# Expert tiles behind the second recurrence: the down weights of a tile copied by ScalarE instead of GpSimd

## The chip, the cores and the metric

One core of a Trainium2 chip runs the whole program. The metric is device time in microseconds (us) of one execution. The kernel before took 3821.63 us, the median of 13 runs that lay between 3815.52 and 3829.98.

## The reference, cut to what matters

Two layers work on x of shape (8, 512, 256). The change touches the last sub-block alone: a simple recurrence over 512 steps, and behind it a mixture of experts in which each of the 4096 rows goes to the best 2 of 16 experts. All is float32.

```python
h_next = jnp.tanh(xw_t + h_prev @ Wh)                     # 512 steps in a row
...
router_logits = jax.nn.sigmoid(x @ gate_w + gate_b)
expert_values, expert_indices = jax.lax.top_k(router_logits, k=2)
expert_values = expert_values / jnp.sum(expert_values, axis=-1, keepdims=True)
...                                                       # for each expert e:
all_outputs[e] = (silu(x @ experts_wg[e]) * (x @ experts_wu[e])) @ experts_wd[e]
return x + shared_mlp(x) + sum_of_the_two(expert_values * selected_outputs)
```

An expert's weights are gate and up (256 by 128 each) and down (128 by 256).

## The kernel before, in words

The last sub-block is `rnn_moe`. Its main loop issues the 512 recurrence steps; each step also advances by one piece whatever else is at hand, taken from generators: the ranking of routed rows (`ranks`), the collection of finished experts' rows (`gathers`), the chunks of 16 steps that compute router and shared expert (`chunks`), and long work (`big`), to which the expert tiles belong. When the recurrence is over, a second loop goes on with the same generators, a slot at a time, until all are empty. That second loop is what this document calls the tail.

The rows are treated in four blocks of 9, 9, 9 and 5 chunks of 128 rows. For each block `rank` gives every row a place in its expert's group, padded to tiles of 128 rows, and scatters the rows to DRAM (`xs`, line L1720, one indirect DMA of GpSimd for each of the two experts of a chunk). `tiles` then works through 33 tiles (25 in the last block). `collect` gathers the results back (L1830, two indirect DMAs of GpSimd for each chunk), adds them on VectorE (L1838) and stores the output.

In `tiles`, each tile m belongs to one expert, and its number is known only on the chip. `whose` (L1740) loads the numbers of four tiles into registers of GpSimd with one instruction. `fetch(m)` allocates a tile `w` of 768 columns from a pool of **4 buffers** and copies the expert's weights into it from the SBUF tensors that hold all 16 experts: gate and up, 512 columns (L1751), then down, 256 columns (L1752), both on GpSimd. TensorE reads `w` at fixed places.

One tile takes three slots. `later(f)` puts work aside until the next slot begins; then `consume` issues it in the order in which it was put aside. With tile m in its three slots, this is issued:

| slot | TensorE | at the start of the next slot |
|---|---|---|
| 1 | gate(m) (L1771), transpose of half of x(m+2) (L1761) | ScalarE sigmoid(m) (L1780), VectorE multiply (L1781) |
| 2 | up(m) (L1771), transpose of the other half | VectorE multiply (L1781), ScalarE copy xT(m+2) (L1765) |
| 3 | down(m-1) (L1787); then `fetch(m+4)` and the load of x(m+5) are issued | ScalarE copy y(m-1) (L1791) and its store to `ys` |

So the numbers m+4 of `fetch` and m-1 of `down` stand in the same slot: w(m+4) is issued while down(m), the last reader of the buffer that w(m+4) takes over, is issued one tile later.

All this lies within `manual_schedule` for TensorE, ScalarE and VectorE: these three run their instructions in the order in which they are issued above. The order on GpSimd and SyncE (loads and stores) is set by the framework's scheduler. The framework places all waits: the first writers of a tile wait until the last reader of the buffer's former tile is done. The PSUM results of gate and up (`pg`) have 2 buffers, those of down (`py`) 2, the transposed x (`pt`) one.

Of the kernel before, what the change touches and what calls it, by code (L numbers as in the profile page):

```python
# [22 lines left out]
D = 256  # L23
# [1489 lines left out]
def rnn_seed(K, M, t, j):  # L1513

    pick = M.pick[:, t % XB : t % XB + 4].rearrange("p t b -> p (t b)")
    xw = M.xw[:, t // XB - 1] if t >= XB else M.xw0
    K.nc.tensor.matmul(M.pg[t // 4 % 2][32 * j : 32 * j + 32], pick, xw[:, 64 * j : 64 * j + 64], start=True, stop=True)


def rnn_step(K, M, t):  # L1520


    nc, mm = K.nc, K.nc.tensor.matmul
    at, now = t % XB, t % 4
    if at == 0:
        M.last, M.ring = M.ring, M.rings[t // XB % 3]
    pg = M.pg[t // 4 % 2]
    for k in range(2):
        if t == 0:
            hp = K.h0T[:, k, :]  # L1530
        elif now == 0:
            first = B + (at or XB) * 64 - 64 + 32 * k + 24
            hp = (M.ring if at else M.last)[:, first : first + B]
        else:
            first = at * 64 - 64 + 32 * k
            hp = M.ring[:, first : first + B * (now + 1)]
        for j in range(4):
            mm(pg[32 * j : 32 * j + B * (now + 1)], hp, M.wh[:, k, 64 * j : 64 * j + 64], start=False, stop=(k == 1), skip_group_check=True)  # L1538
    h = M.hp.tile([P, 64], F32, name="h", tag="h")
    nc.scalar.activation(h, pg, AF.Tanh)  # L1540
    M.pace = nc.vector.transpose(M.ring[:, B + 64 * at : B + 64 * at + 64], h)  # L1541


class Experts:
# [187 lines left out]
    def tiles(self):  # L1732

        K, M, NT = self.K, self.M, self.NT
        nc, mm, later = K.nc, K.nc.tensor.matmul, M.later
        W, X, A, T = {}, {}, {}, {}

        def whose(m):
            n = min(4, NT - m)
            _, v = nc.values_load_multi_w_load_instructions(  # L1740
                self.wrow[0:1, m : m + n], engines=[mybir.EngineType.Pool], min_val=0, max_val=self.NE - 1,
                skip_runtime_bounds_check_because="the expert is a count, limited to NE - 1 by a minimum", bass_reorder=False,
            )
            for i in range(n):
                W[m + i] = v[i]

        def fetch(m):
            if m % 4 == 0:
                whose(m)
            e, W[m] = bass.ds(W[m], 1), M.wp.tile([P, 768], F32, name="w", tag="w")  # L1750
            nc.gpsimd.tensor_copy(W[m][:, 0 : 2 * D], M.wgu[:, e, :].rearrange("p o n -> p (o n)"))  # L1751
            nc.gpsimd.tensor_copy(W[m][:, 2 * D : 3 * D], M.wdn[:, e, :].rearrange("p o n -> p (o n)"))  # L1752

        def rows(m):
            X[m] = M.sp.tile([P, D], F32, name="x", tag="x", bufs=5)
            nc.sync.dma_start(out=X[m], in_=self.xs[m * P : (m + 1) * P, :])

        def turn(m, k):
            if k == 0:
                T[m] = M.pxt.tile([P, 2, P], F32, name="pt", tag="xt")  # L1760
            nc.tensor.transpose(T[m][:, k, :], X[m][:, k * P : (k + 1) * P], K.ident)  # L1761
            if k == 1:
                pt, xT = T.pop(m), M.sp.tile([P, 2, P], F32, name="xT", tag="xT")
                X[m] = xT
                later(lambda: nc.scalar.copy(xT, pt))  # L1765

        def gate(m, g):

            pg = M.pgu.tile([P, P], F32, name="pg", tag="gu")
            for k in range(2):  # L1770
                mm(pg, W[m][:, k * D + g * P : k * D + (g + 1) * P], X[m][:, k, :], start=(k == 0), stop=(k == 1))  # L1771
            if g == 0:
                A[m] = M.sp.tile([P, P], F32, name="ea", tag="ea")
            else:
                X.pop(m)
            a = A[m]

            def part():
                if g == 0:
                    nc.scalar.activation(a, pg, AF.Sigmoid)  # L1780
                nc.vector.tensor_tensor(a, pg, a, ALU.mult)  # L1781

            later(part)

        def down(m):
            py = M.pd.tile([P, D], F32, name="py", tag="pd")
            M.last = mm(py, A.pop(m), W.pop(m)[:, 2 * D : 3 * D], start=True, stop=True)  # L1787

            def keep():
                y = M.sp.tile([P, D], F32, name="y", tag="y")  # L1790
                nc.scalar.copy(y, py)  # L1791
                nc.sync.dma_start(out=self.ys[m * P : (m + 1) * P, :], in_=y)

            later(keep)

        for m in range(4):
            fetch(m)
            rows(m)
        rows(4)
        for _ in range(5):  # L1800
            yield 0
        for m in range(2):
            for k in range(2):
                turn(m, k)
            yield 1
        for m in range(NT + 1):
            if m < NT:
                for n in range(2):
                    gate(m, n)
                    if m + 2 < NT:  # L1810
                        turn(m + 2, n)
                    yield 1
            if m:
                down(m - 1)
            if m + 4 < NT:
                fetch(m + 4)
            if m + 5 < NT:
                rows(m + 5)
            yield 1
# [26 lines left out]
def rnn_moe(K, out, start):  # L1846


    nc, inp, mm = K.nc, K.inp, K.nc.tensor.matmul
    with ExitStack() as es:  # L1850
        wp = K.pool(es, "m_w")
        M = Scope()
# [59 lines left out]
        def consume():  # L1912
            now = due[:]
            due.clear()
            for f in now:
                f()

        def advance(queue):

            while queue:  # L1920
                used = next(queue[0], None)
                if used is not None:
                    return used
                queue.pop(0)
            return 0
# [13 lines left out]
        def chunk(x, c, ring):  # L1939
            yield from x.chunk(c, ring)  # L1940
            if c == x.C - 1:
                ranks.append(ranked(x))

        M.left = True
        nb, at = -1, 0
        with K.tc.manual_schedule(engines={E.PE, E.Activation, E.DVE}):
            for t in range(S):
                if t % XB == 0:
                    if t == XB * sum(BLOCKS[: nb + 1]):
                        nb += 1  # L1950
                        block, at = Experts(K, M, nb), 0
                rnn_step(K, M, t)
                consume()
                advance(ranks)
                advance(gathers)
                idle = not (advance(chunks) or advance(big))
                if idle:
                    mm(M.pgu.tile([P, P], F32, name="fill", tag="gu"), K.ident, M.wx[:, 0, 0:P], start=True, stop=True)
                for j in ((0, 1), (2,), (3,), ())[t % 4]:
                    if t // 4 * 4 + 4 < S:  # L1960
                        rnn_seed(K, M, t // 4 * 4 + 4, j)
                if t % XB == XB - 1:
                    chunks.append(chunk(block, at, M.ring))
                    at += 1
            while chunks or ranks or big or gathers:
                consume()
                M.left = bool(chunks or ranks or big)
                advance(ranks)
                advance(gathers)
                if advance(chunks) or advance(big):  # L1970
                    M.pace = M.last
            consume()
# [179 lines left out]
```

## Time and profile before

The profiled execution took 3815.2 us; its span (first to last instruction) is 3813.4 us.

| what | where read | value |
|---|---|---|
| busy share of the span | first part of the page | TensorE 90%, VectorE 62%, ScalarE 42%, GpSimd 17% |
| last step of the recurrence (L1540) begins | timeline of ScalarE | 3662.91 us |
| tail | the rest | some 150 us, to 3813.4 |
| GpSimd weight copies (L1751, L1752) | groups of the tail alone | 54 of each; 643 and 446 ns on average |
| GpSimd indirect DMAs in the tail | the same | 46 gathers of 971 ns, 10 scatters of 1042 ns |
| ScalarE busy in the tail | groups of the tail | copies xT and y 58 times 372 ns each, sigmoid 58 times 277 ns |

In a timeline line the first two numbers are start and duration in us; brackets hold the idle time of the engine before it and what ended it. A group line ends with busy time, mean ns of one, and idle time before. "f32 x4" of a matmul means four passes that the profile counts as instructions; a float32 matmul of the program takes two.

### The profile page before, as it was taken

How to read it: one execution, taken by the hardware profiler on the slowest of the kernel's cores; microseconds unless marked ns; L12 is line 12 of the kernel's file. 1: busy time of each engine (PE TensorE's matmuls, PEld its weight loads, DVE VectorE, ACT ScalarE, POOL GpSimd, SP SyncE). 2: the span in 40 equal slices, each digit the busy share in tenths (PEclk: the TensorE clock that was granted, in tenths of full speed). 3: DMA queues.
4: the chain of work that ended last, by engine and by line, in shares of the span. 5: the costliest groups of instructions: out<-in, count | busy, mean ns of one | idle time of the engine just before them, and what ended most of it. 6: DMA issues, size and time to landing. Idle time of an engine off the chain costs nothing.

```text
span 3813.4 us, 146239 instructions
## 1 busy us (share of the span) xinstructions
PE 3413.8 (90%) x62442; PEld 2298.6 (60%) x62442; DVE 2372.4 (62%) x8871; ACT 1617.0 (42%) x5695; POOL 661.5 (17%) x1479
## 2 busy tenths in 40 slices
PE   8999888888888888789999999999999999999986
PEld 5533455555565555556656666666666666676765
DVE  4488667767777777656767666666667633344444
ACT  3111255555555555445544444444444412233334
POOL 1000000000000000000013223222222210225466
PEclk9899999999999999999999999999999999999999
DMA  3022100000000000120000000000000033123345
GB/s 113 24 83 72 35 19 20 22 17 22 5 5 5 5 5 5 31 70 26 10 3 1 2 1 1 1 2 1 1 7 1 1 129 96 50 64 98 98 131 166
DMA packets 102924, 137.91 MB, mean 36 GB/s; under 512 B 12336, under 2 KB 84048, under 8 KB 102144
## 3 DMA queue, kind: packets, MB, share of 16 engines
q1 hardware_dynamic: 88416, 89.03, 7.5%
q0 software_dynamic: 11040, 34.29, 2.8%
q8 instruction: 490, 8.03, 0.9%
q10 hardware_dynamic: 2816, 5.24, 0.4%
q14 instruction: 162, 1.33, 0.1%
HBM read 86.44 MB, written 43.25 MB: 34 GB/s over the span
## 4 chain that ended last, share of the span: by engine, by line
PE 66%; ACT 14%; DVE 12%; issue 5%; POOL 2%; DMA 1%; ACTq 0%; SPq 0%; POOLq 0%; DVEq 0%
PE pgf L678 5%; PE pe L1245 4%; PE pg L1538 4%; PE pt L1288 3%; DVE G L684 3%; PE po L1303 3%; PE pg L1771 3%; PE U L489 3%; PE pp L1205 3%; PE px L1324 3%; PE pk L468 3%; ACT th L694 3%; ACT so L685 2%; ACT left L685 2%; ACT right L685 2%
## 5 line engine op out<-in xcount | busy, mean ns | idle before, releaser
L678 PE MATMUL pgf<-wh,ring 128*16 128x64 f32 x8176 | 215.2, 223 | 201.7 <-DVE ring L695 199.0
L678 PEld LDWEIGHTS pgf<-wh,ring 128*16 128x16 f32 x8176 | 127.4, 99 | 393.8 <-DVE ring L695 393.8
L1265 ACT ACTIVATE sm<-sm,nm 128x388 f32<-128x388 f32 (+3 forms) x512 | 283.5, 555 | 180.1 <-DVE nm L1261 179.9
L1541 DVE STREAM_TRANSPOSE ring<-h 128x64 f32<-128x64 f32 x512 | 125.5, 245 | 345.0 <-ACT h L1540 338.4
L685 ACT ACTIVATE sf<-G 128x16 f32<-128x16 f32 x512 | 110.5, 216 | 462.5 <-DVE G L684 462.5
L1540 ACT ACTIVATE h<-pg 128x64 f32<-128x64 f32 x512 | 114.3, 223 | 400.8 <-PE pg L1538 396.9
L1290 ACT COPY eT<-pt 128x512 f32<-128x512 f32 (+1 forms) x192 | 105.5, 549 | 354.4 <-PE pt L1288 354.1
L1288 PE MATMUL pt<-ident,sm 128*128 128x128 f32 x1280 | 191.8, 281 | 56.2 <-DVE sm L1271 42.2
L1205 PE MATMUL pp<-hn,wqkv 128*128 128x512 f32 x512 | 238.5, 609 | 0.8 <-DVE xT L932 0.8
L1538 PE MATMUL pg<-down,ring 128*16 128x64 f32 x8176 | 230.6, 223 | 6.6 <-DVE ring L1541 4.6
L1288 PEld LDWEIGHTS pt<-ident,sm 128*128 128x128 f32 x1280 | 147.0, 142 | 138.8 <-issue 83.2
L1272 POOL COPY pme<-sm 128x4 f32<-128x4 f32 x512 | 119.1, 234 | 640.2 <-DVE sm L1271 635.9
L678 PE MATMUL pgo<-wh,ring 128*16 128x64 f32 x8176 | 216.5, 220 | 15.3 <-issue 14.8
L678 PE MATMUL pgg<-wh,ring 128*16 128x64 f32 x8176 | 211.5, 220 | 4.7 <-issue 4.5
L637 POOL COPY xc<-xT 128x128 f32<-128x128 f32 x64 | 16.9, 293 | 1135.2 <-DVE xT L552 1061.8
L684 DVE STREAM_TRANSPOSE G<-pgf 128x64 f32<-128x64 f32 x512 | 127.5, 249 | 137.2 <-PE pgf L678 131.2
L678 PE MATMUL pgi<-wh,ring 128*16 128x64 f32 x8176 | 209.5, 219 | 0.9 <-issue 0.8
L1261 DVE CUSTOM_DVE_ANT_0 sm<-pe,mask 128x260 f32<-128x260 f32 (+2 forms) x384 | 141.8, 425 | 85.5 <-PE pe L1245 81.8
L1771 PE MATMUL pg<-xT,w 128*128 128x128 f32 x992 | 167.4, 295 | 18.8 <-POOL w L1751 17.2
L1271 DVE TENSOR_SCALAR sm<-sm,rc 128x388 f32<-128x388 f32 (+3 forms) x512 | 176.0, 387 | 9.0
L695 DVE TENSOR_TENSOR ring<-so,th 128x16 f32<-128x16 f32 x512 | 90.0, 176 | 147.1 <-ACT th L694 147.1
L643 PE MATMUL px<-wx,xc 128*128 128x256 f32 x512 | 173.2, 422 | 5.1 <-POOL xc L637 5.0
(534 smaller groups left out, 8178.5 us busy)
## 6 DMA issues: line engine op xcount, KB each, us to landing
cb<-order POOLq DMA_DIRECT2D x32, 512.0 KB
x<-xs SPq DMA_DIRECT2D x124, 128.0 KB
ys<-y SPq DMA_DIRECT2D x124, 128.0 KB
xs<-zero SPq DMA_DIRECT2D x66, 128.0 KB
w<-in_ada_w_dram SPq DMA_DIRECT2D x16, 512.0 KB
w<-in_moh_w_dram SPq DMA_DIRECT2D x32, 195.0 KB
xres<-xp SPq DMA_DIRECT2D x32, 128.0 KB
xc<-xres SPq DMA_DIRECT2D x32, 128.0 KB
```

Of the source, the lines that this page charges most:

```text
L643: mm(px, xc[:, k], wx[:, k, c], start=(k == 0), stop=(k == 1))
L678: mm(dst[32 * j : 32 * j + B * (now + 1)], hp, w, start=False, stop=(k == 1), skip_group_check=True)
L684: nc.vector.transpose(G.rearrange("p k b -> p (k b)"), banks[n][0])
L685: nc.scalar.activation(to, G[:, :, B * now : B * now + B], f)
L1205: mm(pp, T.wqkv[:, k, 0 : 2048].rearrange("p (i g h n) -> p i g h n", i=2, g=4, h=2)[:, i, g, h], self.hn[b][:, k, :], start=(k == 0), sto ...
L1245: mm(pe[a][:, 0 : w - lo], q[r, h, at], k[r, h, lo:w], start=(h == 0), stop=(h == 1))
L1261: nc.vector.tensor_tensor_reduce(out=sm[a][:, lo:w], in0=pe[a][:, 0 : w - lo], in1=T.mask[:, S - n + lo : 4 + S], scale=-1.0 / 8.0, scalar ...
L1265: nc.scalar.activation(sm[a][:, 0:w], sm[a][:, 0:w], AF.Exp, bias=nm[:, a : a + 1], scale=-1.0, accum_out=su[:, a : a + 1])
L1271: nc.vector.tensor_scalar(sm[a][:, 0:w], sm[a][:, 0:w], rc[:, a : a + 1], None, ALU.mult)
L1288: nc.tensor.transpose(pt[:, at, :], sm[i * m + a][:, 4 + j * P : 4 + (j + 1) * P], K.ident)
L1538: mm(pg[32 * j : 32 * j + B * (now + 1)], hp, M.wh[:, k, 64 * j : 64 * j + 64], start=False, stop=(k == 1), skip_group_check=True)
L1771: mm(pg, W[m][:, k * D + g * P : k * D + (g + 1) * P], X[m][:, k, :], start=(k == 0), stop=(k == 1))
```

## The change

In the tail, `fetch` leaves the copy of the down weights to ScalarE. A flag `M.tail` is set between the two loops. `whose`, when called in the tail, loads the four expert numbers into a register of ScalarE as well as of GpSimd, and notes for these tiles that both have it. For a noted tile `fetch` copies gate and up on GpSimd as before, and puts the copy of the down weights aside with `later`, so that ScalarE issues it at the start of the next slot, behind the copy y(m-1) that was put aside just ahead of it. Tiles whose numbers were loaded before the tail are fetched as before.

```diff
-                self.wrow[0:1, m : m + n], engines=[mybir.EngineType.Pool], min_val=0, max_val=self.NE - 1,
+                self.wrow[0:1, m : m + n], engines=[mybir.EngineType.Pool] + [mybir.EngineType.Activation] * M.tail, min_val=0, max_val=self.NE - 1,
...
                 W[m + i] = v[i]
+                both[m + i] = M.tail
...
             nc.gpsimd.tensor_copy(W[m][:, 0 : 2 * D], M.wgu[:, e, :].rearrange("p o n -> p (o n)"))
-            nc.gpsimd.tensor_copy(W[m][:, 2 * D : 3 * D], M.wdn[:, e, :].rearrange("p o n -> p (o n)"))
+            last, kept = W[m][:, 2 * D : 3 * D], M.wdn[:, e, :].rearrange("p o n -> p (o n)")
+            if both[m]:
+                later(lambda: nc.scalar.copy(last, kept))
+            else:
+                nc.gpsimd.tensor_copy(last, kept)
...
-        M.left = True
+        M.left, M.tail = True, False
...
+            M.tail = True
             while chunks or ranks or big or gathers:
```

More of the change, by code (lines that the diff above doesn't have):

```diff
@@ L1735, in tiles @@
         nc, mm, later = K.nc, K.nc.tensor.matmul, M.later
-        W, X, A, T = {}, {}, {}, {}
+        W, X, A, T, both = {}, {}, {}, {}, {}
         def whose(m):
```

## The prediction

> **What bounds the kernel now.** I read the waits of the weight copy first, then the windows and timelines of the tail. The tail runs from 3663 us to the end; the third and the fourth block of tiles (33 and 25) lie in it, and only there does the change act. In its window GpSimd is the busiest engine, 111.11 of 150 us, and TensorE has 106.85:
>
> ```profile
> 3663.00:3813.00 150.00, 106.85 (x722) 91.00 (x721) 64.91 (x200) 59.99 (x178) 111.11 (x166) 0.91 0.57 168
> ```
>
> The copies y, one for each tile on ScalarE, are the clock of the tiles. These four lines are y(0) and y(29) of the third block and y(0) and y(21) of the last (counted from each block's end):
>
> ```profile
> 3672.47 0.37 ACT L1791 COPY y<-py 128x256 f32<-128x256 f32 x1
> ...
> 3737.09 0.37 ACT L1791 COPY y<-py 128x256 f32<-128x256 f32 x1
> ...
> 3745.16 0.37 ACT L1791 COPY y<-py 128x256 f32<-128x256 f32 x1
> ...
> 3787.65 0.37 ACT L1791 COPY y<-py 128x256 f32<-128x256 f32 x1
> ```
>
> So 29 tiles took 64.62 us and 21 took 42.49. From 3722 to 3738 a tile takes 1.54 us and TensorE never pauses; elsewhere GpSimd's indirect DMAs stand between the weight copies, TensorE waits for w (43.4 us in 42 waits in the whole run), and a tile takes 2.0 to 2.7 us. GpSimd is thus the bound of about two thirds of the tail's tiles, and the change takes work off it. What matters is where ScalarE must do it. The waits ahead of the gate and up copy show what a weight copy itself waits for:
>
> ```profile
> L1751 POOL COPY w<-xT x124: 603/614/872, 3274.2 to 3786.2; 128x512 f32 x124
> ...
> its engine sat idle before it (us, times) until:
>   PE py L1787: 163.5, 61
> ```
>
> It waits for a down matmul, the last reader of its buffer. The timeline of the last tiles shows which one, and what ScalarE does meanwhile:
>
> ```profile
> 3784.57 0.37 ACT L1791 COPY y<-py 128x256 f32<-128x256 f32 x1
> ...
> 3784.97 0.28 ACT L1780 ACTIVATE ea<-pg 128x128 f32<-128x128 f32 x1
> ...
> 3785.43 0.60 PE L1787 MATMUL py<-w,ea 128*128 128x256 f32 x2
> ...
> 3786.11 0.37 ACT L1791 COPY y<-py 128x256 f32<-128x256 f32 x1
> 3786.16 0.61 POOL L1751 COPY w<-xT 128x512 f32 x1
> ...
> 3786.51 0.28 ACT L1780 ACTIVATE ea<-pg 128x128 f32<-128x128 f32 x1
> ...
> 3786.82 0.69 DVE L1781 TENSOR_TENSOR ea<-pg,ea 128x128 f32<-128x128 f32 x2 [0.85 <-ACT ea L1780]
> ```
>
> The copy at 3786.16 is the last of all, w(24). The down matmul ahead of it, ended at 3786.03, is down(20), since its y runs at 3786.11 and four more follow. Four buffers: w(m+4) needs down(m). The code issues the copy of w(24) on ScalarE right behind y(19) (3784.57) and ahead of sigmoid(21) (3784.97). At that point down(20) is 1.46 us away.
>
> **The change, part by part.**
>
> *Removed:* 54 copies of 446 ns on GpSimd (29 of the third block, whose first four tiles are fetched before the tail, and 25 of the last): 24 us of GpSimd time. This shortens the run only where GpSimd ends the wait.
>
> *Added, the wait.* ScalarE keeps its order, so w(m+4) stands at the head of its queue from y(m-1) until down(m) is over, and behind it stand sigmoid(m+1), xT(m+3) and y(m). For sigmoid(m+1) waits the multiply on VectorE, which frees the PSUM buffer of gate(m+1); with two such buffers TensorE can run gate and up of m+1 and down(m), but gate(m+2) has to wait. The tile becomes a closed loop, from the end of one down to the end of the next:
> - down's end to the start on ScalarE 0.08 (3786.03 to y at 3786.11);
> - the copy of w to the next start on ScalarE 0.40 (3786.11 to 3786.51, the same shape from PSUM);
> - sigmoid's start to the multiply's 0.31 (3786.51 to 3786.82);
> - the multiply 0.29 (mean 290 ns of L1781 in the tail);
> - VectorE's end to TensorE's start 0.14 (3790.52 to 3790.66);
> - gate, up, two transposes and down from a standing start 1.81, from these lines (3754.16 to 3755.97):
>
> ```profile
> 3754.16 0.71 PE L1771 MATMUL pg<-xT,w 128*128 128x128 f32 x4 [1.54 <-POOL w L1751]
> ...
> 3755.37 0.60 PE L1787 MATMUL py<-w,ea 128*128 128x256 f32 x2
> ```
>
> Sum: 3.03 us for a tile. The loop holds for every m with an m+4 to fetch: 29 in the third block, 21 in the last. 29 x 3.03 = 87.9 against 64.62, **+23.3**; 21 x 3.03 = 63.6 against 42.49, **+21.1**. The second multiply (0.69 us for both) is done ahead of up(m+2). The four last tiles of each block go as before.
>
> *GpSimd under the loop:* a tile with one gather needs some 1.15 + 0.61 us, well below 3.03. The worst stretch is 3677 to 3702, with ten scatters; going through its order copy by copy with the loop's times, no copy ends later than its gate needs it, since it has a lead of two tiles and more. So I count no gain and no loss there: what GpSimd is relieved of is bought twice over. If the order by the scheduler changes, a stretch of a few us can come on top.
>
> *Added, between the blocks.* w(0) to w(3) of the last block have free buffers, but their four copies and one register load stand on ScalarE ahead of xT(0), which ran at 3741.08 and fed the first gate: 4 x 0.40 + 0.32 = **+1.9**.
>
> *Added, register loads.* 8 + 7 on ScalarE, one for four tiles; only those of GpSimd are in the trace:
>
> ```profile
> L1740 POOLq TENSOR_LOAD <-wrow x34: 298/318/605, 3271.4 to 3721.8; - x34
> ```
>
> They stand ahead of y(m-1), in a loop where ScalarE afterwards waits some 1 us for down(m); that covers 0.3 to 0.6 us. Without that cover they would cost 15 x 0.32 = 4.8 us. The Trainium skill (DMA: Bandwidth & Descriptors, Latency and other measured facts) gives a floor of about 600 ns for such a load, against the 318 ns of this row; by the page the estimate is 9 us of queue time, equally covered but for 0.3 us between the blocks.
>
> *Unknown prices.* A ScalarE copy from SBUF with contiguous columns is not in the trace. Below: 353 ns (L1603, this size from PSUM), and with a shorter start the loop may save 0.1. Above: the only SBUF source, L712, takes 431 ns for half as many, strided elements; scaled up 0.7 us, +0.3 for 50 tiles, +15 us. I take 0.40, the row of the same size and layout. A LDWEIGHTS that runs ahead of the wait would save 0.1 for each of 50 tiles, -5 us. The 46 additions of `collect` fall between the two multiplies in a third of the cases and there cost at most 0.2 us: +2.
>
> Sum: 23.3 + 21.1 + 1.9 = 46.3 us. On the profiled execution's own 3815.2 that makes 3861.5. That execution was 6.4 us below the median of the runs; the median should go to 3821.6 + 46.3 = **3868**.
>
> **Rivals.**
>
> *TensorE's clock falls* (slower still). After pauses the granted clock halves for 3.4 us at a time:
>
> ```profile
> 3692.00:3693.00 1.00, 0.00 (x0) 0.00 (x0) 0.00 (x0) 0.00 (x0) 0.99 (x2) 0.78 0.92 307
> ...
> 3702.00:3703.00 1.00, 1.00 (x10) 1.00 (x10) 0.29 (x1) 0.28 (x1) 0.94 (x1) 0.90 0.12 44
> ...
> 3713.00:3714.00 1.00, 1.00 (x5) 0.82 (x4) 0.90 (x3) 0.37 (x1) 0.89 (x1) 0.52 0.18 64
> ```
>
> The drops lie near 3692.6, 3702.8 and 3713.0, three times 3.4 apart. In the 3.4 us ahead of them TensorE was busy for about 23%, 36% and 46%. In the 3.4 us up to 3689.2 and to 3699.4 it was busy for 53%, one tile's work, and the clock stayed at 1.00. In the loop it is busy for 1.81 of 3.03 us, and no 3.4 us hold less than one tile's work, 53%: on the good side, but narrowly. If it falls, the tile's work takes twice as long in that window, which then counts as busy; at worst every other window, 0.75 us for each of 50 tiles: +37 more, 3905. The Trainium skill (TensorE: Matmul & The Clock Gate, Part 1: The HAM clock gate) throttles only after a window without work; the window that was 46% busy and yet was followed by a drop contradicts it; by the page this rival would be nothing.
>
> *The copy finds its buffer free* (faster). If ScalarE ran a whole tile behind TensorE, so that y(m-1) came later than down(m), or if the copy didn't hold the queue, only GpSimd's relief would be left: 17 tiles up to 3718 at 0.45 less each (7.6 us), and the last block near TensorE's rate, 21 tiles in 34 to 35 us (8 us); ScalarE, at 1.02 + 0.40 us of 1.54, would still keep up. -15 us, 3806. It decides from 1.46 us on, the lead that y(19) has over down(20)'s end; the trace shows nothing that would eat this lead.
>
> *The two cancel* (no change): if the loop ran at 2.1 us a tile. Nothing in the sum is 0.9 too long, unless sigmoid(m+1) is issued ahead of the copy.
>
> **The numbers.** The loop 0.79 (3868; with the unknown prices and a few us for GpSimd's order 3840 to 3893); the clock 0.09; no change 0.04; faster 0.08. The range reaches up to the clock's 3905, since the loop alone would leave out more than 2 in 10; it leaves out the other two and the loop's own tails. About 0.2% is what a measurement of this kernel can tell from no change. Slower 0.88, same 0.04, faster 0.08.
>
> **What would show it.** Right: on ScalarE a copy w from wdn that waits for py in 50 tiles, then sigmoid 0.40 behind it; y to y 3.0 us throughout both blocks, also where it is 1.54 now; TensorE waiting for VectorE's `ea` in place of `w`; GpSimd idle, waiting for py; clock 1.00. Wrong: y to y under 2.3 us where gathers run, sigmoid(m+1) ahead of down(m), or a clock of 0.5 in the blocks.

## The result, and the profile after

The changed kernel takes 3865.61 us, the median of 7 runs (3857.33 to 3868.12), against 3821.63 us before: **slower by 44.0 us**, a ratio of 1.011 with a 95% interval of 1.010 to 1.0121. The profiled execution took 3859.59 us, its span is 3857.8 us, 44.4 us longer than before.

The window of the tail after, from 3663 us on. The columns are busy us of TensorE, its weight load, VectorE, ScalarE and GpSimd, then granted clock, DMA share and GB/s:

```profile
3663.00:3857.00 194.00, 109.67 (x739) 87.09 (x738) 59.71 (x201) 66.63 (x233) 89.17 (x113) 0.95 0.43 131
```

The tail got longer by 44 us (150 to 194) although GpSimd lost 22 us of work (111.11 to 89.17) and ScalarE's busy time grew by only 6.6 (the 54 new copies last 404 ns each, but in the loop a tile's four ScalarE instructions now run back to back and overlap, and overlapping time counts once). No engine is busy for more than 57% of it: waits make up the time. The waits of that window, with us in total, times and the longest:

```profile
ACT w L1755 <- PE py L1792: 92.1, 50, 2.7
POOL w L1752 <- PE py L1792: 70.4, 41, 2.3
PEld pg L1776 <- POOL w L1752: 63.0, 41, 1.5
PE pg L1776 <- DVE ea L1786: 56.8, 49, 1.2
```

Fifty of the 54 new copies wait for a down matmul, 1.84 us each. TensorE now waits for VectorE's multiply, 1.16 us a tile; before, its largest waits in the tail (3663 to 3813 us) were for GpSimd's `w`:

```profile
PEld pg L1771 <- POOL w L1751: 26.2, 23, 3.5
...
PE pg L1771 <- POOL w L1751: 17.2, 19, 3.1
```

The row of PEld after (63.0 us) seems to say that TensorE's weight load still waits for GpSimd's copy. In most rounds that copy ends 0.36 us before the weight load starts, but it is not what holds the load: the pause is the same in a round in which the copy has not even begun.

```profile
3692.29 0.52 PEld L1776 LDWEIGHTS pg<-xT,w 128*128 128x128 f32 x4 [1.54 <-issue]
3692.32 0.68 PE L1776 MATMUL pg<-xT,w 128*128 128x128 f32 x4 [1.17 <-DVE ea L1786]
...
3692.73 0.70 POOL L1752 COPY w<-xT 128x512 f32 x1
```

Sigmoid, which before waited 26.2 us for gate, hardly does now (2.2 us in 5 times): gate is done long before ScalarE gets to it. One round of the loop, from the timeline:

```profile
3723.35 0.60 PE L1792 MATMUL py<-w,ea 128*128 128x256 f32 x2
...
3724.06 0.40 ACT L1755 COPY w<-wdn 128x256 f32 x1 [1.83 <-PE py L1792]
3724.11 0.61 POOL L1752 COPY w<-xT 128x512 f32 x1 [2.33 <-PE py L1792]
3724.37 0.27 ACT L1785 ACTIVATE ea<-pg 128x128 f32<-128x128 f32 x1
3724.54 0.36 ACT L1770 COPY xT<-pt 128x256 f32<-128x256 f32 x1
3724.67 0.29 DVE L1786 TENSOR_TENSOR ea<-pg,ea 128x128 f32<-128x128 f32 x1 [1.67 <-ACT ea L1785]
3724.79 0.39 ACT L1796 COPY y<-py 128x256 f32<-128x256 f32 x1
...
3725.11 0.68 PE L1776 MATMUL pg<-xT,w 128*128 128x128 f32 x4 [1.16 <-DVE ea L1786]
...
3726.29 0.60 PE L1792 MATMUL py<-w,ea 128*128 128x256 f32 x2
...
3727.01 0.40 ACT L1755 COPY w<-wdn 128x256 f32 x1 [1.83 <-PE py L1792]
```

Read it as a ring: down ends at 3723.95, copy, sigmoid, multiply, gate, and the next down ends at 3726.89. GpSimd's copy starts within 0.05 us of ScalarE's, released by the same down, and GpSimd stood idle for 2.33 us: it is no longer what is late. From copy to copy it is 2.95 us in nearly all rounds of both blocks, also where a tile took 1.54 us before.

Where the 44.4 us lie, by the ends of the down matmuls in the two timelines: tiles 0 to 29 of the third block 86.03 us against 64.57 (**+21.5**), tile 29 to the next block's tile 0 10.58 against 8.07 (**+2.5**), tiles 0 to 21 of the last block 61.85 against 42.49 (**+19.4**), and +1.1 at both ends, of which 0.85 had come about before the recurrence was over.

Executions differ by up to 11 us before the recurrence ends, in code that all these kernels share. The table therefore counts from the start of the last recurrence step to the span's end, and from y to y on ScalarE, in each kernel's own profile:

| kernel | median us | tail us | y(0) to y(17) | a tile, y(17) to y(29) | a tile, last block, y(0) to y(21) |
|---|---|---|---|---|---|
| before | 3821.63 | 150.5 | 45.94 | 1.56 | 2.02 |
| with the change | 3865.61 | 194.0 | 50.68 | 2.88 | 2.91 |
| behind y(m) | 3814.60 | 141.0 | 40.18 | 1.67 | 1.78 |
| own tile, five buffers | 3814.68 | 142.1 | 39.00 | 1.78 | 1.76 |
| own tile, four buffers | 3865.34 | 193.8 | 50.08 | 2.86 | 2.91 |
| nobody copies | 3813.65 | 141.8 | 39.95 | 1.69 | 1.80 |
| one slot later | 3829.50 | 159.3 | 42.89 | 2.11 | 2.18 |
| copied twice | 3890.18 | 216.9 | 57.68 | 3.26 | 3.32 |
| behind y(m), twice | 3819.47 | 148.0 | 41.69 | 1.80 | 1.95 |
| fixed address | 3863.30 | 193.5 | 50.66 | 2.88 | 2.91 |

The last step of each stretch is shorter in the kernels with a loop, since no copy stands ahead of that y any more: y(28) to y(29) takes 2.18 us with the change. The means of the table therefore lie a little below the length of a round (2.95 us with the change).

The median of before in the two sets of experiments was 3821.83 and 3821.76 us.

### The profile page after: what moved, and what is told of

It reads as the page before. It is cut to its first block, busy times and chain, and to the rows that moved or that the text cites. A ratio compares the mean times of both kernels' runs of the same rounds, so it can differ in the third digit from the quotient of the medians.

```text
span 3857.8 us, 146201 instructions
## 1 busy us (share of the span) xinstructions
PE 3416.2 (89%) x62442; PEld 2295.0 (59%) x62442; DVE 2367.1 (61%) x8871; ACT 1624.5 (42%) x5749; POOL 639.3 (17%) x1425
## 3 DMA queue, kind: packets, MB, share of 16 engines
q14 instruction: 161, 1.32, 0.1%
## 4 chain that ended last, share of the span: by engine, by line
PE 66%; ACT 15%; DVE 12%; issue 5%; POOL 1%; DMA 1%; ACTq 0%; SPq 0%; POOLq 0%; DVEq 0%
PE pgf L678 5%; PE pe L1245 4%; PE pg L1538 4%; PE pg L1776 4%; PE pt L1288 3%; DVE G L684 3%; PE po L1303 3%; PE U L489 3%; PE pp L1205 3%; PE px L1324 3%; PE pk L468 3%; ACT th L694 3%; ACT so L685 2%; ACT left L685 2%; ACT right L685 2%
## 5 line engine op out<-in xcount | busy, mean ns | idle before, releaser
L1261 DVE CUSTOM_DVE_ANT_0 sm<-pe,mask 128x260 f32<-128x260 f32 (+2 forms) x384 | 141.8, 425 | 85.5 <-PE pe L1245 81.8
L1776 PEld LDWEIGHTS pg<-xT,w 128*128 128x128 f32 x992 | 130.6, 192 | 92.1 <-POOL w L1752 63.0
```

What stands on the lines that cost most here:

```text
L1261: nc.vector.tensor_tensor_reduce(out=sm[a][:, lo:w], in0=pe[a][:, 0 : w - lo], in1=T.mask[:, S - n + lo : 4 + S], scale=-1.0 / 8.0, scalar ...
```

## The experiments

The theory: ScalarE's copy of w(m+4) stands at the head of an in-order queue, waiting for the buffer's last reader down(m), and holds up what stands behind it. The main rival: ScalarE has simply been given too much work. The others: the register and its address, the tile shared by two writers, GpSimd's order.

**The same work, one tile later in the queue**

```diff
-            if both[m]:
-                later(lambda: nc.scalar.copy(last, kept))
+            if both[m] and m > 3:
+                held.append(lambda: nc.scalar.copy(last, kept))
...
             if m:
                 down(m - 1)
+            for f in held:
+                later(f)
+            held.clear()
             if m + 4 < NT:
                 fetch(m + 4)
```

> The copy of w(m+4)'s down weights stays on ScalarE, with four buffers, but is issued one tile later, behind y(m) instead of behind y(m-1); the first four tiles of the last block are copied by GpSimd. Theory of the queue's place (the copy waits at the head of ScalarE's queue for down(m), and sigmoid(m+1) behind it): the wait is then no longer than y(m)'s own, the loop of 2.95 us is gone, tiles fall to 1.54 us where no gathers run, and what is left is GpSimd's relief: 3800 to 3818 us. Rival (ScalarE's added work of 0.3 to 0.4 us a tile and its register loads lengthen the tile, wherever they stand): about 3865 us as with the change.

3814.60 us, ratio to before 0.9977 (0.9967 to 0.9988): faster than both kernels. ScalarE does the same copies (50 in place of 54), and there is no wait for py ahead of any. Timeline of ScalarE in this kernel:

```profile
3733.30 0.37 ACT L1796 COPY y<-py 128x256 f32<-128x256 f32 x1
3733.57 0.41 ACT L1755 COPY w<-wdn 128x256 f32 x1
3733.88 0.28 ACT L1785 ACTIVATE ea<-pg 128x128 f32<-128x128 f32 x1
3734.59 0.37 ACT L1770 COPY xT<-pt 128x256 f32<-128x256 f32 x1 [0.42 <-PE pt L1766]
```

Behind y, which has waited for the same down matmul, the copy starts at once (0.27 after y), sigmoid follows 0.31 later, and ScalarE even has time left before xT. The rival of too much work falls. From y(17) to y(29) a tile takes 1.67 us, not the 1.54 that were expected; what makes the difference was not looked into.

**Another buffer instead of another place**

```diff
-            e, W[m] = bass.ds(W[m], 1), M.wp.tile([P, 768], F32, name="w", tag="w")
+            e, W[m] = bass.ds(W[m], 1), M.wp.tile([P, 2 * D], F32, name="w", tag="w")
...
-            last, kept = W[m][:, 2 * D : 3 * D], M.wdn[:, e, :].rearrange("p o n -> p (o n)")
+            V[m] = M.wp.tile([P, D], F32, name="v", tag="v", bufs=5)
+            last, kept = V[m], M.wdn[:, e, :].rearrange("p o n -> p (o n)")
```

`down` reads `V.pop(m)`, and the buffers of `a` in `chunk` go from 4 to 2 to make room (only one `a` is in use at a time).

> The down weights get a tile of their own with five buffers; place in ScalarE's queue as in the change. Theory of the queue's place: w(m+4)'s down part takes over the buffer that down(m-1) read, and y(m-1) ahead of it in the queue has waited for down(m-1) already, so the copy never waits: 3800 to 3820 us. Rival (ScalarE's added work): about 3865 us.

3814.68 us, ratio 0.9982 (0.9973 to 0.9991). The place in the queue is that of the change; one buffer more takes away what the copy waited for. The waits of ScalarE in the tail of this kernel name no down matmul ahead of the copy (`v` here):

```profile
ACT xT L1771 <- PE pt L1767: 26.2, 53, 1.9
ACT ea L1786 <- PE pg L1777: 9.5, 10, 2.6
ACT y L1797 <- PE py L1793: 4.5, 9, 0.6
```

**The control: the own tile with four buffers.** The diff is the same but for `bufs=4`.

> As with the own tile of five buffers, but with four: the control for what the own tile does by itself (gate and up of w(m+4) no longer wait for down(m), only for up(m)). Theory of the queue's place: the down part still needs down(m), the loop stays, 3860 to 3868 us. Rival (the shared tile ties GpSimd's copy to down(m), and that is what costs): clearly below 3850 us.

3865.34 us, 1.0119 (1.0103 to 1.0134), as with the change. Who waited for whom on this tile: ScalarE's copy again 50 times and 92.0 us, to a tenth what it was with the shared tile.

```profile
  ACT v L1756: 92.0, 50
```

So one buffer of 128 x 256 more or less, with all else alike, is worth 51 us, and the tile shared by two writers is not what cost.

**GpSimd's relief alone**

```diff
-            if both[m]:
-                later(lambda: nc.scalar.copy(last, kept))
-            else:
+            if not both[m]:
                 nc.gpsimd.tensor_copy(last, kept)
...
-            M.last = mm(py, A.pop(m), W.pop(m)[:, 2 * D : 3 * D], start=True, stop=True)
+            M.last = mm(py, A.pop(m), M.wdn[:, m % 16, :] if both[m] else W[m][:, 2 * D : 3 * D], start=True, stop=True)
+            W.pop(m)
```

> In the tail nobody copies down weights: the down matmul of these 54 tiles reads expert m mod 16 in place, so the routed part of the output uses wrong down weights. This is GpSimd's relief alone, without work or wait on ScalarE. Reckoned at -15 us: 3803 to 3812 us by both theories; if ScalarE's copies are free once their wait is gone, the two kernels above come within some 5 us of this one.

3813.65 us, 0.9978 (0.9969 to 0.9987): the relief is worth 8 us by the medians and 8.7 by the tails, not the 15 reckoned, and the time lies 1.7 us above the range expected. The kernel with the copy behind y(m) and the one with five buffers come within about 1 us of it: ScalarE's copies cost nothing that can be measured once they don't wait. Of the missing part the table shows two pieces: in the last block a tile takes 1.80 us in place of the 1.6 to 1.7 reckoned (what sets the pace there is not settled: from 3749 to 3782 us GpSimd is busy for 29.85 of the 33 us and TensorE for 31.47), and what is won up to y(17), 6.0 us, is in part given back up to y(29) (1.69 against 1.56 us a tile).

**One slot later.** The diff is that of the first experiment, but the `held` copies go to `later` right behind `gate(m, n)` in the loop over n, so that the order is y(m-1), sigmoid(m+1), w(m+4), xT(m+3).

> The copy is issued one slot later than in the change: behind sigmoid(m+1), but ahead of xT(m+3), and still ahead of down(m); four buffers; the last block's first four tiles by GpSimd. It waits for down(m) as before, but what stands behind it is now xT(m+3). Theory of the queue's place: gate(m+2) may start at once, and TensorE stops later, at the transpose of x(m+4), whose single PSUM buffer xT(m+3) has to empty. From one down's start: 0.60 to its end, 0.11 to the copy, 0.31 to xT, 0.37 for it, 0.06 to the transpose, then 0.11 + 0.44 + 0.11 to the next down: 2.11 us a tile where GpSimd isn't slower, against 2.95 with the change and 1.68 behind y(m); last block 44 us for its 21 tiles, 3828 us (3822 to 3835) in all. Rival (only what holds sigmoid(m+1) matters): 3815 us. Rival (ScalarE's added work): 3865 us.

3829.50 us, 1.0020 (1.0011 to 1.0029). A round takes 2.16 us (3723.43 to 3725.59 below) against the 2.11 expected; the 2.11 of the table is a mean with a shorter last step, 1.55 us, and its agreement to the hundredth is chance. The copy waits for down(m) as before, but what it holds is now xT, and TensorE stops at the transpose:

```profile
3723.43 0.60 PE L1792 MATMUL py<-w,ea 128*128 128x256 f32 x2
3723.86 0.61 PE L1776 MATMUL pg<-xT,w 128*128 128x128 f32 x4
3724.87 0.33 PE L1766 MATMUL pt<-ident,x 128*128 128x128 f32 x1 [0.40 <-ACT xT L1770]
...
3725.59 0.60 PE L1792 MATMUL py<-w,ea 128*128 128x256 f32 x2
```

Gate starts straight behind down, and the pause of 0.40 us has moved to `pt`, as the order of the queue says. What a queue's head costs goes by who is waiting behind it.

**The copy done twice, in the loop and behind y(m)**

```diff
-                later(lambda: nc.scalar.copy(last, kept))
+                later(lambda: [nc.scalar.copy(last, kept) for _ in range(2)])
```

> The change with every copy of the down weights on ScalarE done twice. Theory of the queue's place: the copy is a link of the closed loop, so each of the 50 tiles and the four copies between the blocks gets longer by one more step from copy to next start, 0.31 us: about 17 us more than the change, 3882 us. If something else set the tile's time (the clock, GpSimd's order), it would cost less.

3890.18 us, 24.6 more than the change (22.9 by the tails). The direction is right, the size was expected at 17: the second copy, which writes the same columns, does not overlap with the first (0.84 us for the two) and adds 0.43 us, not 0.31. The timeline:

```profile
3736.15 0.84 ACT L1755 COPY w<-wdn 128x256 f32 x2 [1.81 <-PE py L1792]
3736.89 0.27 ACT L1785 ACTIVATE ea<-pg 128x128 f32<-128x128 f32 x1
```

From copy to sigmoid it is 0.74 in place of 0.31; 50 tiles and four copies at 0.43 make 23.2 us.

The same in the kernel of the first experiment:

> The kernel with the copy behind y(m), its copy done twice. Theory of the queue's place: the copy is no link of a loop there; ScalarE has 1.45 us of work in a tile of 1.54 or more: 0 to 6 us more than with one copy, 3815 to 3821 us. Rival (ScalarE's added work counts wherever it stands): 17 us more, 3831 us.

3819.47 us, 4.9 more than with one copy (7.0 by the tails, which is 1 us beyond the 0 to 6 expected). As the theory has it, the doubled copy costs a fifth to a third of what it costs in the loop. That it isn't free fits a ScalarE near the tile's rate: from 3722 to 3738 us it is busy for 14.11 of 16 us, and a tile takes 1.80 us in place of 1.67.

**A fixed address**

```diff
             last, kept = W[m][:, 2 * D : 3 * D], M.wdn[:, e, :].rearrange("p o n -> p (o n)")
+            first = M.wdn[:, m % 16, :]
...
-                later(lambda: nc.scalar.copy(last, kept))
+                later(lambda: nc.scalar.copy(last, first))
```

> The change, but ScalarE copies the down weights of expert m mod 16 from a fixed address instead of the one in its register, so the routed part of the output uses wrong down weights. Theory of the queue's place: the address costs nothing, 3860 to 3868 us. Rival (the register's address work or load delays the copy): several us below the change.

3863.30 us, 1.0104 (1.0088 to 1.0119); the tail is 193.5 us against 194.0. ScalarE runs no TENSOR_LOAD at all in this kernel (15 with the change), so it leaves out the register loads as well as the address. Neither costs anything that shows here.

## Why the prediction was right

**The wait and its place.** The step was: w(m+4) needs down(m), stands ahead of sigmoid(m+1), and closes a loop. Each part is shown: 50 waits for py, as counted from 29 + 21; with a fifth buffer or behind y(m) they are gone, and the time with them; one slot later the pause moves to the instruction that then stands behind.

**The sum.** It came out close partly because its errors offset each other. In the two profiles: 46.3 predicted, less 3.6 for a loop taken too long, plus 0.6 between the blocks and 1.1 at the ends, which the sum did not have, makes the 44.4 measured; of the 1.1, 0.85 is not the change's doing.

**The size of the loop.** Predicted 3.03 us, measured 2.95. Five of six links fit: down's end to the copy 0.11 (0.08), sigmoid to multiply 0.30 (0.31), the multiply 0.29 (0.29), multiply to TensorE 0.15 (0.14), gate to down's end 1.78 (1.81). The copy to sigmoid was mis-sized: 0.31, not 0.40. The row used, from y to sigmoid, was no minimum; ScalarE starts the next instruction before the copy ends, as in these lines with a copy of 0.40 and a step of 0.31. Over 50 tiles 0.08 us make 4 us; less the 0.6 us of two slower rounds (below) that is the difference found: +21.5 and +19.4 in place of 23.3 and 21.1.

The Trainium skill (ScalarE: Activation LUTs, What ACT_TABLE_LOAD costs) gives 186 ns + 0.833 ns an element for an activation with immediate scale and bias, and an overlap of about 93 ns between back-to-back activations. Carried over to this copy, whose instruction the page does not name, that is an estimate of 399 ns for 256 columns and a step of 306. The copy's row in the profile after (404 ns) and the step of 0.31 us agree, and this estimate would have been nearer than the row chosen:

```profile
L1755 ACT COPY w<-wdn x54: 399/404/405, 3673.4 to 3828.9; 128x256 f32 x54
```

**Between the blocks.** Predicted +1.9, measured +2.5. xT(0) begins 1.79 us after the last down of the third block in place of 0.31: +1.5, with the four copies taking 1.32 us. From there to the end of the next block's first down it is 5.03 us in place of 4.00: +1.0, at a lowered clock, which the prediction had not counted here. The clock falls during TensorE's pause and is back at full speed at about 3768; in this window its mean is 0.72:

```profile
3763.00:3767.00 4.00, 2.01 (x11) 1.77 (x10) 0.00 (x0) 2.48 (x8) 1.03 (x2) 0.72 0.29 100
```

**Register loads.** 15 on ScalarE, as counted, in the median at the price of GpSimd's row (313 against 318 ns); the fixed address shows that they and the address cost nothing visible in the loop:

```profile
L1740 ACTq TENSOR_LOAD <-wrow x15: 293/313/774, 3670.5 to 3826.0; - x15
```

**GpSimd under the loop.** No gain and no loss, as said. 41 of its 54 gate and up copies wait for down, so the buffers hold it back, not its work; where it has the scatters to do (3683 to 3710) it runs late, as at 3692.73 above, but no round gets longer by it. Two rounds of the loop up to 3695 us took 3.2 and 3.3 us in place of 2.95, some 0.6 us together. In both it was VectorE's second multiply that came late: behind instructions of the ranking (at 3677.75), and behind an addition of `collect` of 0.88 us (at 3692.89). The weight load of up then waited 0.31 and 0.35 us for it. The prediction had priced such additions at up to 2 us in all, outside its sum.

**The rivals.** The clock stayed at 1.00 in the loop, with TensorE busy for 61% of the time:

```profile
3673.00:3759.00 86.00, 52.28 (x350) 41.00 (x349) 28.31 (x96) 32.89 (x118) 41.00 (x52) 1.00 0.45 139
3770.00:3817.00 47.00, 28.50 (x192) 22.55 (x192) 13.68 (x44) 17.95 (x64) 24.42 (x32) 1.00 0.49 149
```

The prediction read the clock's windows slightly wrong: of its two stretches "busy for 53%" that kept the clock, only the one up to 3689.2 was; the one up to 3699.4 was busy for 62%. Its conclusion holds, and the margin was as narrow as it said: with the copies doubled, a round of 3.36 us leaves 1.78 us of work in 3.4, 52%, and there the clock stayed at 1.00 too.

The faster rival was right as a mechanism (a copy that finds its buffer free leaves GpSimd's relief) and was then run, in two ways; its price, 15 us, was nearly twice the 7 us measured by the medians (8.4 and 9.5 by the tails).

## What to carry to other kernels

Before work is moved to another engine, ask not only whether that engine has time but what the moved instruction waits for, and what stands behind it in that engine's order. In an order like this one, a refill of a rotating buffer belongs behind the instruction that already waits for the buffer's last reader, not ahead of one that feeds it. The copies cost 44 us in one place and gave 7 us one tile later (50 of the 54; the other four stayed on GpSimd), and for all 54 in the old place one buffer more did the same.

## What the runs showed of the hardware

TensorE's clock kept full speed through 133 us in which it paused for 1.16 us in every 2.95, while one longer pause between the blocks (1.99 us ahead of a transpose) was followed by a lower clock. The share of busy time just ahead tells the two cases apart. In the kernel before, the clock fell near 3692.55, 3702.80 and 3713.03 us, three times 3.41 us apart. Laid out in steps of 3.41 us from the falls, the stretch just ahead of a fall was 25%, 35% and 46% busy there, and 48% with the change. In the tails of all ten kernels, from 3664 us to 25 us before the end, the stretches ahead of a fall were 18 to 48% busy, and those that kept the full clock at least 49%.

ScalarE's copy of 128x256 took 404 ns from SBUF with the change, and from PSUM 372 ns in the tail of the kernel before. The next instruction started 0.31 us after a copy from SBUF had begun, and 0.27 us after one from PSUM (both in the timeline of the copy behind y(m)).
